# Gathers of two experts' rows moved ahead, and the copy of x to the output in other places, in a fused conditional-linear and mixture-of-experts kernel

## The chip, the core and the metric

The kernel runs on one core of one Trainium2 chip. The metric is the device time of one execution in microseconds (us), and a kernel's time is the median of its runs. Five engines work side by side, each through its own instructions in order: PE (matrix multiply; PEld is its weight load), DVE (elementwise, reductions), ACT (activations, copies), POOL (here mostly indirect DMAs) and SP (here only the issue of DMAs). Each waits for the others by semaphores. DMAs issued by SP, ACT and POOL stand in separate queues and are carried by the same 16 DMA engines. Matrix products are summed in PSUM, everything else lies in SBUF, and inputs, outputs and intermediates in device memory (DRAM).

## The reference, cut to what matters

```python
# x: (4, 1024, 512); per batch row b a category c = itok[b]
xc = einsum('bsd,bdh->bsh', x, W[c]) + b[c]          # conditional linear, (4096, 512)
probs = softmax(xc @ Wr)                             # 8 experts
eidx = argmax(probs); p_tok = probs[eidx]
rank = position of the token among those of its expert   # kept if rank < 512
for e in range(8):                                   # dispatch[e]: up to 512 token numbers
    h  = maximum(xc[dispatch[e]] @ W1[e], 0)         # 512x512 times 512x2048
    ye = (h @ W2[e]) * p_tok                         # 512x2048 times 2048x512
    y[dispatch[e]] += ye
out = x + y
```

All is float32. A token that no expert keeps has `out = x`; a kept token has `out = x + p * ye`.

## The kernel before

**The front (the first 147 us).** The four batch rows are taken in turn. For each, x is loaded in tiles of 512 tokens (`load_x`, L248), turned by PE (`transpose_x`, L268), and multiplied by the category's weight (`load_batch`, L206; `linear`, L473). All products use Strassen's scheme: seven products of half blocks, whose sums and differences DVE forms before and after. The result is written to two DRAM tensors, `xc_dram[0]` and `[1]`, the left and right 256 columns (`done`, L512). Beside it the router picks the expert and the rank of each token; POOL scatters the pairs (probability, token) to `slots` in DRAM, which ACT's queue loads back as `table` (L644), and POOL makes the index tables `src_row` and `dst_row` from it (L651). The loads at the start, all in the order of the program: x tile 0 on ACT's queue (L625), then `wr_sb` (L627) and the zeroing of `slots` (L630) there; on SP's queue the weight of batch row 0 in three pieces (L214), x tile 1, the weight of row 1, x tile 2, the weight of row 2.

**The experts.** Each of the eight experts takes some 95 us. `gather` (L691) brings in rows by indirect DMAs on POOL, in two uses: from pool `xg` (one buffer) the expert's 512 rows of xc, eight DMAs, `rows_of`; from pool `xr` (four buffers) its 512 rows of x itself, four DMAs, `rows`, called the residual here. `fetch(e)` (L711) copies the indices to `at` on DVE and gathers the rows of expert e+1 and the residual of expert e. It is called in `between` (L956) at the second of four groups of hidden columns (g = 1), held behind the latest sum on DVE by `behind`. The rows of expert 0 are gathered at the start of the expert part (L980) and turned on PE (`transpose_rows`, L761). The rows of the later experts are turned without PE: ACT copies them into `strips` (`regroup`, L736, 16 copies), then DVE transposes 32x32 blocks (`turn`, L749) and forms their differences (`sum_xe`, L727).

The first layer (`first_layer`, L781, matmuls L787) makes the hidden values `h` with ReLU on ACT (L807, L814). The second layer (`second_layer`, L840, matmuls L848) makes three big products, k = 1, 6 and 7, into one PSUM bank in turn; the four others are split once more (`inner_product`, L896, matmuls L901). `add` (L828) multiplies a product by the probability and adds it to the residual row (DVE, L833). So product k = 6 cannot write the bank before `add` has read k = 1 out of it, and `add` needs the residual. The last 8 of the 32 matmuls of k = 6 need the last group's sums of `h` (DVE, L163 to L166). The finished rows are scattered to `out` on POOL (L946), and a row buffer of `xr` is free once its scatter has landed.

**The copy of x to the output.** Tokens without an expert need `out = x`, so x is copied to `out` from DRAM to DRAM, 8 MB, before the first scatter. It is in three parts on SP's queue in expert 0, at g = 1, 2 and 3 (L974 to L977), between the loads of the first-layer weights (`load_w1`, L177). `load_w2` (L669) loads an expert's second-layer weight, 4 MB, on the same queue.

**What sets the order.** Inside `tc.manual_schedule` the instructions of PE and SP stand in the order of the program. Those of DVE, ACT and POOL are placed by a scheduler that estimates when each can start; `high_priority` and `issue_after` bend its choice. Each DMA raises one of eight semaphores of its kind, in turn, and a DMA waits until the one before it on its semaphore has landed.

Of the kernel before, what the change touches and what calls it, by code (L numbers as in the profile page):

```python
# [16 lines left out]
P = 128  # L17
# [5 lines left out]
def kernel(  # L23
# [11 lines left out]
    nc = tc.nc  # L35
# [3 lines left out]
    T = B * S  # L39
# [7 lines left out]
    SC = CAP // P  # L47
# [4 lines left out]
    NG = F // (2 * HB * P)  # L52
# [6 lines left out]
    xf = x.rearrange("b s d -> (b s) d")  # L59
    of = out.rearrange("b s d -> (b s) d")  # L60
# [4 lines left out]
    xg = ctx.enter_context(tc.tile_pool(name="xg", bufs=1))  # L65
# [14 lines left out]
    def behind(f, *at):  # L80

        with tc.issue_after(latest[0].ins):
            f(*at)
# [51 lines left out]
    xc_dram = [dram.tile([T, HD], F32, name=f"xc{j}_dram") for j in range(2)]  # L135

    table = const.tile([P, SC, E, ROW], F32, name="table")
    src_row = const.tile([P, NS], I32, name="src_row")
# [53 lines left out]
    with (  # L192
# [55 lines left out]
        def load_x(c, eng=nc.sync):  # L248
            t = xin.tile([P, XT, D], F32, tag="x", name=f"x_{c}")
            n = 1 if c == 0 else XT  # L250
            for j in range(0, XT, n):
                eng.dma_start(
                    out=t[:, j : j + n, :],
                    in_=xf[c * CT + j * P : c * CT + (j + n) * P, :].rearrange(
                        "(j p) d -> p j d", p=P
                    ),
                )
            xrows[c] = t

        def behind_this(f):  # L260
            with tc.issue_after(latest[0].ins):
                latest[0] = f()
# [210 lines left out]
        def linear(b, g, k):  # L473
# [145 lines left out]
            (1, 8): [(load_x, 7)],  # L619
            (1, 12): [(load_w1, 0, 1)],  # L620
            (2, 3): [(load_w1, 0, 2)],
        }

        with tc.manual_schedule(engines={mybir.EngineType.PE, mybir.EngineType.SP}):
# [3 lines left out]
                out=wr_sb[:, :, 0:E], in_=wr.rearrange("(kc p) e -> p kc e", p=P)  # L628
# [16 lines left out]
            out=table.rearrange("p c e r -> p (c e r)"),  # L645
            in_=slots.rearrange("(p s) r -> p (s r)", p=P),
# [13 lines left out]
    xr = ctx.enter_context(tc.tile_pool(name="xr", bufs=SC, reuse_waits="tile"))  # L660
# [6 lines left out]
    rows, residual, xes, hs = {}, {}, {}, {}  # L667
# [23 lines left out]
    def gather(e, pool, sources, into, at):  # L691

        n = D // len(sources)
        if pool is xg:
            into[e, "all"] = pool.tile([P, SC, D], F32, tag="rows", name=f"rows_of_{e}")
        for j, source in enumerate(sources):
            for c in range(SC):
                if pool is xg:
                    into[e * SC + c] = into[e, "all"][:, c, :]
                elif j == 0:  # L700
                    into[e * SC + c] = pool.tile(
                        [P, D], F32, tag="rows", name=f"rows_{e * SC + c}"
                    )
                nc.gpsimd.indirect_dma_start(  # L704
                    out=into[e * SC + c][:, j * n : (j + 1) * n],
                    out_offset=None,
                    in_=source,
                    in_offset=bass.IndirectOffsetOnAxis(ap=at[:, c : c + 1], axis=0),
                )
# [71 lines left out]
    def first_layer(e, g, k):  # L781

        key = (1, e, g)
        ps = bank(ps_p, key, k, [P, HB, HC * P], "h", bufs=2)
        for j in range(HB):
            for kc in range(HK):
                nc.tensor.matmul(  # L787
                    ps[:, j, :],
                    lhsT=w1s[e, g][:, LEFT[k], kc, j * P : (j + 1) * P],
                    rhs=xes[e][:, RIGHT1[k], kc, :],  # L790
                    start=(k in OPENS and j == 0 and kc == 0),
                    stop=(k == LAST[BANK[k]] and j == HB - 1 and kc == HK - 1),
                    skip_group_check=True,
                )
        if e not in hs:
            hs[e] = hp.tile([P, NG, 7, HB, HC * P], F32, tag="h", name=f"h_{e}")
        h = hs[e][:, g, :, :, :]
        if k in (1, 6, 7):
            banks[key, k] = snap.tile(
                [P, HB, HC * P], F32, tag=f"s{k}", bufs=1 + (k == 6), name=f"s{k}_{e}_{g}"  # L800
            )
            snapped[0] = nc.scalar.copy(banks[key, k], ps)  # L802

        def total(into, ps, part):
            with tc.high_priority():
                latest[0] = nc.vector.tensor_tensor(into, ps, part, ALU.add)  # L806
            nc.scalar.activation(into, into, AF.Relu)  # L807

        if k == 2:
            total(h[:, 0, :, :], ps, banks.pop((key, 1)))  # L810
        if k == 7:
            total(h[:, 3, :, :], banks[key, "y"], banks.pop((key, 7)))
        if k == 4:
            nc.scalar.activation(h[:, 1, :, :], ps, AF.Relu)  # L814
        if k == 3:
            total(h[:, 2, :, :], ps, banks.pop((key, 6)))
            sums(nc.vector, *(h[:, i, :, :] for i in range(7)))
# [138 lines left out]
    def between(e, g):  # L956

        if g == 0 and e > 0:
            behind(sum_w1, e, W1G - 2)
        if g > 0:  # L960
            if e > 0 or g > 2:
                first_layer(e, g - 1, 4)
                first_layer(e, g - 1, 3)
            ahead = e * NG + g - 1 + W1G
            if ahead < E * NG:
                load_w1(*divmod(ahead, NG))
            if ahead > W1G and ahead <= E * NG:
                behind(sum_w1, *divmod(ahead - 1, NG))
        part = g - 2 + (e == 0)
        if part in (0, 1):  # L970
            behind(sum_w2, e, part)
        if g == 1:
            behind(fetch, e)
        if e == 0 and g > 0:  # L974

            q = slice((g - 1) * T // (NG - 1) // P * P, g * T // (NG - 1) // P * P)
            nc.sync.dma_start(out=of[q, :], in_=xf[q, :])  # L977

    with tc.manual_schedule(engines={mybir.EngineType.PE, mybir.EngineType.SP}):
        gather(0, xg, xc_dram, rows, src_row)  # L980

        for part, half, then in (
            (0, 0, [(0, 1)]),
            (0, 1, [(1, 1), (0, 5), (1, 5)]),
            (1, 0, [(0, 2)]),
            (1, 1, [(1, 2)]),
        ):
            for c in range(half * HC, (half + 1) * HC):
                transpose_rows(0, c, part)
            for g, k in then:  # L990
                first_layer(0, g, k)

        load_w2(0, xes[0][:, 3, 0, HC * P - 1 :])
        for e in range(E):
            for g in range(NG):
                if e == 0 and g < 2:

                    for k in ((6, 7), (4, 3))[g]:
                        first_layer(e, 0, k)
                        first_layer(e, 1, k)  # L1000
                    between(e, g)
                    continue
                first_layer(e, g, 1)
                first_layer(e, g, 2)
                ahead = range(0 if 0 < e < E - 1 and g == NG - 1 else VB, VB)
                for a in ahead[:1]:
                    regroup(e + 1, a)
                between(e, g)
                for i, k in enumerate((6, 5, 7)):
                    first_layer(e, g, k)  # L1010
                    for a in ahead[i + 1 : i + 2]:
                        regroup(e + 1, a)
            second_layer(e, 1)
            first_layer(e, NG - 1, 4)
            inner_sums(e, 2, sides="right")
            first_layer(e, NG - 1, 3)
            inner_sums(e, 2, sides="left")
            if (e + 1) * NG - 1 + W1G < E * NG:
                load_w1(e + 1, W1G - 1)
            if e == 0:  # L1020

                for a in range(VB):
                    regroup(1, a)

            def small(*turns):
                for k, q in turns:
                    inner_product(e, k, q)

            second_layer(e, 6)
            inner_sums(e, 5)  # L1030
            small(*[(2, q) for q in (1, 5, 2, 6, 3, 7)])
            second_layer(e, 7)
            small((2, 4))
            inner_sums(e, 3)
            inner_sums(e, 4)
            if e + 1 < E:
                turn(e + 1)
            small((5, 5), (5, 2))
            if e + 1 < E:
                sum_xe(e + 1)  # L1040
            small(
                *[(5, 1), (5, 3), (5, 6), (3, 5), (5, 7), (3, 2), (5, 4), (3, 1)],
                *[(4, 5), (4, 1), (3, 6), (4, 2), (4, 6)],
                *[(3, 3), (4, 3), (3, 7), (4, 7), (3, 4), (4, 4)],
            )
            if e + 1 < E:
                load_w2(e + 1)
# [31 lines left out]
```

## Time and profile before

| | us |
|---|---|
| median of 3 runs | 930.53 (929.09 to 930.55) |
| the profiled execution | 935.05 |
| its span, first to last instruction | 933.3 |
| PE busy | 907.0 (97%) |
| DVE busy | 660.2 (71%) |
| ACT busy | 264.1 (28%) |
| POOL busy | 177.6 (19%) |

The profiled execution lies 4.5 us above the median, and 1.75 us of it lie around the span. Times below that name a moment are us from the start of the span. PE is the engine to watch: where it neither multiplies nor waits for its own queue, the kernel stands. The granted clock of PE is listed with the stretches; 1.00 is full speed.

### The profile page before, as it was taken

Reading aid. Unit: us, or ns where it says so; the run is one execution under the profiler, and the core shown is the slowest. Engines: PE = TensorE matmul, PEld = TensorE weight load, DVE = VectorE, ACT = ScalarE, POOL = GpSimd, SP = SyncE. Lnnn points to the kernel's source line nnn. Section 1 sums busy time; section 2 is a strip of 40 time slices with the busy share of each in tenths; the row PEclk is TensorE's granted clock in tenths of the full one; section 3 lists DMA queues with packets and bytes.
Section 4 is the critical chain, followed back from the end, with each engine's and each line's share of the span. In section 5 each row is a group of like instructions: output and inputs, shape, how many; then the busy total and the mean of one; then the engine's idle time right before and its main releaser. Section 6 shows DMA issues by size and latency. Waiting matters only on the chain.

```text
span 933.3 us, 13219 instructions
## 1 busy us (share of the span) xinstructions
PE 907.0 (97%) x5204; PEld 807.8 (87%) x5204; DVE 660.2 (71%) x1226; ACT 264.1 (28%) x506; POOL 177.6 (19%) x173
## 2 busy tenths in 40 slices
PE   9999999986999999999999999999999999999996
PEld 6788787875998899889988998899889988998896
DVE  4656684655946993699469945995599558965893
ACT  3333201315123412351236122602260136013200
POOL 0043343070015001500150015001500150011001
PEclk9999999997999999999999999999999999999999
DMA  9474224991075206520652066205620462135001
GB/s 323 147 232 159 80 92 123 340 376 73 1 241 165 91 1 225 181 91 1 213 187 91 1 201 205 87 5 175 221 71 30 149 227 73 46 120 192 1 1 46
DMA packets 95727, 123.31 MB, mean 132 GB/s; under 512 B 8516, under 2 KB 83268, under 8 KB 95474
## 3 DMA queue, kind: packets, MB, share of 16 engines
q1 hardware_dynamic: 85058, 96.49, 30.9%
q0 software_dynamic: 9216, 24.85, 8.1%
q10 hardware_dynamic: 1392, 1.13, 0.4%
q8 instruction: 41, 0.67, 0.3%
q14 instruction: 20, 0.16, 0.1%
HBM read 105.96 MB, written 25.23 MB: 141 GB/s over the span
## 4 chain that ended last, share of the span: by engine, by line
PE 91%; DVE 3%; DMA 2%; POOL 2%; issue 2%; ACT 1%; POOLq 0%; SPq 0%; DVEq 0%
PE hx L787 22%; PE yx L848 17%; PE yx L901 12%; PE hy L787 11%; PE yy L901 6%; PE xcx_lin L491 6%; PE hz L787 5%; PE yz L901 3%; PE xcy_lin L491 2%; PE xcz_lin L491 1%; POOL rows_of L704 1%; PE ps_xT L276 1%; ACT strips L747 1%; DMA rows<-in_x_dram,at 1%; PE ps_lT L382 1%
## 5 line engine op out<-in xcount | busy, mean ns | idle before, releaser
L787 PE MATMUL hx<-xe,w 128*128 128x256 f32 x1024 | 238.4, 380 | 3.9 <-issue 2.8
L787 PEld LDWEIGHTS hx<-xe,w 128*128 128x128 f32 x1024 | 193.2, 190 | 32.6 <-issue 5.0
L946 POOL DMA_INDIRECT out_dram<-rows,dst_row x32 | 32.0, 999 | 473.5 <-DVE rows L833 421.2
L787 PE MATMUL hy<-xe,w 128*128 128x256 f32 x512 | 120.6, 379 | 0.0
L848 PE MATMUL yx<-w_b,h 128*128 128x256 f32 x512 | 113.1, 379 | 0.0
L802 ACT COPY s<-hx 128x512 f32<-128x512 f32 x96 | 55.7, 580 | 188.5 <-PE hx L787 166.6
L787 PEld LDWEIGHTS hy<-xe,w 128*128 128x128 f32 x512 | 97.3, 190 | 13.2
L848 PEld LDWEIGHTS yx<-w_b,h 128*128 128x128 f32 x512 | 96.7, 190 | 12.8
L806 DVE TENSOR_TENSOR h<-hy,s 128x512 f32<-128x512 f32 x64 | 44.1, 689 | 84.6 <-ACT s L802 38.2
L807 ACT ACTIVATE h<-h 128x512 f32<-128x512 f32 x96 | 60.5, 630 | 114.8 <-DVE h L806 104.3
L704 POOL DMA_INDIRECT rows_of<-xc_dram,at x56 | 63.8, 1140 | 140.7 <-DVE w L164 94.0
L901 PE MATMUL yx<-w_b,h 128*128 128x128 f32 x640 | 84.0, 277 | 0.0
L901 PEld LDWEIGHTS yx<-w_b,h 128*128 128x128 f32 x640 | 79.4, 194 | 1.0
L747 ACT COPY strips<-rows_of 32x512 f32<-32x512 f32 x112 | 69.0, 616 | 16.1 <-DMA rows<-in_x_dram,at 14.7
L848 PE MATMUL yx<-w_t,h 128*128 128x256 f32 x256 | 61.0, 398 | 11.8 <-DVE rows L833 7.1
L848 PEld LDWEIGHTS yx<-w_t,h 128*128 128x128 f32 x256 | 51.2, 201 | 20.1 <-DVE rows L833 7.5
L787 PE MATMUL hz<-xe,w 128*128 128x256 f32 x256 | 60.6, 379 | 0.6 <-DVE xe L769 0.6
L806 DVE TENSOR_TENSOR h<-hz,s 128x512 f32<-128x512 f32 x32 | 22.1, 689 | 54.7 <-PE hz L787 54.7
L787 PEld LDWEIGHTS hz<-xe,w 128*128 128x128 f32 x256 | 48.5, 190 | 7.4 <-DVE xe L769 0.9
L463 POOL DMA_INDIRECT slots<-row,dest x32 | 36.3, 1135 | 95.3 <-DVE dest L459 86.8
L901 PE MATMUL yx<-w_t,h 128*128 128x128 f32 x384 | 51.7, 278 | 0.0
L901 PEld LDWEIGHTS yx<-w_t,h 128*128 128x128 f32 x384 | 46.7, 192 | 0.2
(161 smaller groups left out, 1273.1 us busy)
## 6 DMA issues: line engine op xcount, KB each, us to landing
w<-in_L_ffn_W_dram SPq DMA_DIRECT2D x64, 512.0 KB
w_b<-in_L_ffn_W_dram SPq DMA_DIRECT2D x32, 1024.0 KB
x<-in_x_dram SPq DMA_DIRECT2D x7, 1024.0 KB
xc_dram<-s SPq DMA_DIRECT2D x22, 256.0 KB
out_dram<-in_x_dram SPq DMA_DIRECT2D x2, 2816.0 KB
cw<-in_L_cond_W_dram SPq DMA_DIRECT2D x3, 1024.0 KB
out_dram<-in_x_dram SPq DMA_DIRECT2D x1, 2560.0 KB
xc_dram<-xc SPq DMA_DIRECT2D x8, 256.0 KB
```

Of the source, the lines that this page charges most:

```text
L276: nc.tensor.transpose(ps[:, kc, :], xrows[c][:, j, kc * P : (kc + 1) * P], ident)
L463: nc.gpsimd.indirect_dma_start(out=slots, out_offset=bass.IndirectOffsetOnAxis(ap=dest[:, j : j + 1], axis=0), in_=row[:, j, :], in_offset ...
L491: nc.tensor.matmul(ps[:, j, :], lhsT=left[:, kc, j * P : (j + 1) * P], rhs=right[k][:, kc, :], start=((k in OPENS or (b, k) == (LATE, 3)) ...
L704: nc.gpsimd.indirect_dma_start(out=into[e * SC + c][:, j * n : (j + 1) * n], out_offset=None, in_=source, in_offset=bass.IndirectOffsetOnA ...
L747: nc.scalar.copy(into.rearrange("p k s v -> p s k v"), r[:, :, :, b, :])
L787: nc.tensor.matmul(ps[:, j, :], lhsT=w1s[e, g][:, LEFT[k], kc, j * P : (j + 1) * P], rhs=xes[e][:, RIGHT1[k], kc, :], start=(k in OPENS an ...
L802: snapped[0] = nc.scalar.copy(banks[key, k], ps)
L806: latest[0] = nc.vector.tensor_tensor(into, ps, part, ALU.add)
L807: nc.scalar.activation(into, into, AF.Relu)
L848: nc.tensor.matmul(ps[:, at, :], lhsT=hs[e][:, m // HB, LEFT[k], m % HB, at * P : (at + 1) * P], rhs=w2s[e][RIGHT2[k]][:, m, :], start=(k ...
L901: nc.tensor.matmul(ps, lhsT=left[:, g, :], rhs=right[:, g, :], start=(q in OPENS and g == 0), stop=(q == LAST[BANK[q]] and g == NG - 1), s ...
L946: nc.gpsimd.indirect_dma_start(out=of, out_offset=bass.IndirectOffsetOnAxis(ap=dst_row[:, n : n + 1], axis=0), in_=residual.pop(n), in_off ...
```

## The change

Three things are altered. Expert 0's residual is gathered directly behind the call that gathers its rows, and expert 1's rows behind the first-layer products that follow the turning of expert 0's rows; both read their indices from `src_row`, and `fetch(0)` and its index copy fall away. The copy of x is cut in four parts of 1024 tokens, 2 MB each. The first is written into the plan of the front beside product (2, 5) and issued on ACT's queue. The three others stand on SP's queue after expert 0's first big product and the load of expert 1's third weight block, ahead of `regroup(1)`.

```diff
+        def keep_x(eng, i, n=1):
+
+            q = slice(i * T // 4, (i + n) * T // 4)
+            eng.dma_start(out=of[q, :], in_=xf[q, :])
...
             (2, 3): [(load_w1, 0, 2)],
+            (2, 5): [(keep_x, nc.scalar, 0)],
         }
...
-        if g == 1:
+        if g == 1 and e > 0:
             behind(fetch, e)
-        if e == 0 and g > 0:
-
-            q = slice((g - 1) * T // (NG - 1) // P * P, g * T // (NG - 1) // P * P)
-            nc.sync.dma_start(out=of[q, :], in_=xf[q, :])

     with tc.manual_schedule(engines={mybir.EngineType.PE, mybir.EngineType.SP}):
         gather(0, xg, xc_dram, rows, src_row)
+        gather(0, xr, [xf], residual, src_row)
...
             for g, k in then:
                 first_layer(0, g, k)
+        gather(1, xg, xc_dram, rows, src_row[:, SC : 2 * SC])
...
             if e == 0:
-
+                for i in range(1, 4):
+                    keep_x(nc.sync, i)
                 for a in range(VB):
                     regroup(1, a)
```

## The prediction

> **What bounds the kernel now.** The page gives PE 97% of the span and the chain that ended last 91% PE, so only places where PE stands, or runs slowly, can pay. I went through PE's timeline from the first expert on and compared expert 0 with expert 1, from the first big second-layer product to the next expert's first product. PE's rows (start, duration, count; in brackets the idle time before and what ended it), expert 0:
>
> ```profile
> 195.35 7.07 PE L848 MATMUL yx<-w_b,h 128*128 128x256 f32 x32
> 202.25 1.89 PE L787 MATMUL hx<-xe,w 128*128 128x256 f32 x8
> 203.98 1.89 PE L787 MATMUL hy<-xe,w 128*128 128x256 f32 x8
> 212.94 7.69 PE L848 MATMUL yx<-w_t,h 128*128 128x256 f32 x24 [7.06 <-DVE rows L833]
> 225.32 3.78 PE L848 MATMUL yx<-w_t,h 128*128 128x256 f32 x8 [4.70 <-DVE h L164]
> ...
> 261.94 1.89 PE L787 MATMUL hx<-xe,w 128*128 128x256 f32 x8
> ```
>
> and expert 1, where the same 32 matmuls of k = 6 follow at once:
>
> ```profile
> 307.64 7.07 PE L848 MATMUL yx<-w_b,h 128*128 128x256 f32 x32
> ...
> 318.00 7.07 PE L848 MATMUL yx<-w_t,h 128*128 128x256 f32 x32
> ...
> 356.97 1.89 PE L787 MATMUL hx<-xe,w 128*128 128x256 f32 x8
> ```
>
> Expert 0 takes 66.59 us (261.94 - 195.35), expert 1 49.33: 17.26 us more for the same work. Of these 11.76 are the two idle times (7.06 + 4.70). The rest is a slow clock behind them: the 24 matmuls took 7.69 where 24/32 of 6.91 is 5.18, the 8 took 3.78 for 1.73, and the stretches of 212 to 216 and 224 to 228 us show granted clocks of 0.50 and 0.54.
>
> What is behind the idle times, in the waits from 205 to 226 us (total, times, longest):
>
> ```profile
> ACT strips L747 <- DMA rows<-in_x_dram,at: 14.7, 1, 14.7
> DVE rows L833 <- DMA rows<-in_x_dram,at: 9.2, 2, 8.9
> ...
> DVE xe L754 <- ACT strips L747: 6.9, 1, 6.9
> ```
>
> The first idle time is `add` waiting for expert 0's residual. The second is the 16 `strips` copies, which begin only at 210.87, when the gathers have landed; the transposes on DVE wait for them, and the sums of h stand behind the transposes. The gathers began late (POOL 186.55, held behind DVE's index copy) and then crawled. From 188 to 192 us SP's queue (q1) with its copies of x left POOL's (q0) next to nothing (packets, MB, share of the engines):
>
> ```profile
> q1 hardware_dynamic: 194, 1.82, 109.8%
> q0 software_dynamic: 3, 0.01, 0.7%
> ```
>
> **Step 1, both stalls in expert 0 go.** I read the order of the built program and counted on in the time of before. Residual 0 is issued at about 146 us and expert 1's rows from 160 us on (when PE's last turning of expert 0's rows, at 158.24, frees the one buffer): 8 gathers of about 1.25 (0.95 and 0.30 between) end at 170, some 25 us ahead of their use. `add` then runs at 203, beside PE's two first-layer products (202.25 to 205.71), so k = 6 starts at 205.71 and wants its last 8 matmuls' sums at 205.71 + 5.18 = 210.89. On ACT `strips` starts behind the snapshot ending at 196.19: 3 copies (0.626 each, as 8.14 for 13), a ReLU 0.63, 12 copies 7.51, a ReLU 0.60, one copy 0.61: 207.4. From the last strip to the end of the DVE sum that PE needs (L164) took 225.27 - 222.16 = 3.11 before, so 210.6. That is 0.3 inside. What is late next is thus ACT's strips, with almost no margin; I charge 0.2. Gain **17.26 - 0.2 = 17.1**, and at worst 12 if strips or transposes come 3 to 5 us late and PE's clock drops once more.
>
> **Step 2, the front pays for the first copy.** The plan has it beside product (2, 5), but ACT's order is the scheduler's, and the built program has it in fourth place on ACT: behind the zeroing of `slots` (issued at 3.38) and ahead of ACT's table load (3.76). So it is issued at about 3.8 us. There the DMA engines are full (busy of PE, PEld, DVE, ACT, POOL, then clock, DMA share, GB/s):
>
> ```profile
> 6.00:8.00 2.00, 1.64 (x13) 1.09 (x11) 0.00 (x0) 1.65 (x4) 0.00 (x0) 1.00 0.98 307
> 8.00:10.00 2.00, 1.78 (x8) 1.58 (x9) 0.69 (x1) 0.49 (x2) 0.00 (x0) 1.00 0.99 342
> ...
> 26.00:28.00 2.00, 2.00 (x17) 1.16 (x18) 0.69 (x1) 0.89 (x2) 0.00 (x0) 1.00 1.05 408
> ```
>
> 2.1 MB at the 380 to 410 GB/s of 12 to 28 us is 5.1 to 5.5 us. Its 32 rows of 64 KB are larger pieces than the 44 KB that left q0 0.7%, so I let it hold the engines alone for 5.2 us, from about 7 (ACT's queue still has small packets at 6 to 8), and shift every load on SP's queue by that. The first 256 KB of weights, for which PE waits at 8.22, is just in. The third piece of weights, for which DVE waited 0.91 us until 10.12, comes at 15.3; four DVE operations of 0.61 behind it let PE's third product start at 17.8 in place of 13.53. x tile 1 was first used at 16.38, was in by 15.8 at the latest (SP's next load on its semaphore was issued then), and comes by 21.0 against 16.38 + 4.3 = 20.7. PE is nearly gapless from there to 147 us, so the delay stays: **+4.4**. If the loads keep their share it is 0, and all of 5.2 plus a slow clock is 8.6 at most (rival B).
> x tile 2's load also waits for the copy, which holds the place before it on its semaphore: issued near 14 instead of 9.98 and first used at 31.74, it has room. ACT's own issue (0.66 to 4.70 for the copies before) holds its first copy of `xT` (6.09) 0 to 4 us; PE loses that once, ahead of the weights it waits for anyway.
>
> **Step 3, POOL's new order.** The residual gathers stand between the two halves of expert 0's rows. They wait for the front's last matmul (146.3, its operands lie where the buffers are) and take 4 x 1.25, so the second half, which began at 150.11, starts at 151.35 or, with 1 MB more in the air, 152.5. It was used at 155.18 with no wait. A landing of 2.7 us (last write of `xc_dram` issued by 147.4, seen by POOL at 150.11) gives 155.3 for the second gather that this needs: **+0.6**, 0 to 2.5.
> Then POOL has expert 2's rows ahead of expert 0's scatter, and expert 1's residual behind it. From expert 1's start they came at 17.7 and 28.6 us; now 17.7, scatter 28.6, residual from 33.7 on, landed near 42. Its first `add` is at 52.6 (314.7 - 262.1): hidden by 10 us.
>
> **Step 4, what moves under cover.** The three copies are issued at about 207, take 6.3 MB / 380 GB/s = 17 us while DMA is idle (216 to 260 us: 0 to 4 GB/s), and are done 20 us before `load_w2(1)`. Expert 1's rows (1 MB) now share 160 to 175 us with `load_w2(0)`: about 3 us later, at 178, where DVE first uses it at 178.11, and then w1 of group 3 at 180.5 against its use at 183.25. The index copy (0.16) goes. Cost nothing, at worst 1.
>
> **Sum.** -17.3 + 0.2 + 4.4 + 0.6 = -12.1. The profiled execution becomes 935.05 - 12.1 = 922.9. It stood 4.5 above the median; with the same distance the median is 930.53 - 12.1 = **918.4**.
>
> **A rule weighed.** By the row above a queue beside large copies keeps 0.7%, and the sum goes by it. The Trainium skill, DMA: Bandwidth & Descriptors, section Queues, rings and completion order, has each DMA engine take turns between queues and drain some 9 to 17 descriptors at a turn. An estimate by that page: a turn of 1 KB pieces carries up to 17 KB against 64, so the loads keep a fifth, the weights come 4.2 late in place of 5.2, and the sum would be -13.1.
>
> **Rivals.**
> A: the front's copy costs little (0 to 2), because the loads keep their share or the copy truly runs later. For it: DMA moves 0 GB/s at 38 to 42 us, and the plan names row 2. Against: the built order. Sum -15.7, so 914.8.
> B: the front's stall also slows PE's clock. PE would stand from 10.0 to about 13.8. A 4.70 us idle time was followed by a half clock, and 3.78 and 1.91 for 1.73 and 0.89 is about 3.4 us lost in all. Sum -8.7, so 921.8. The Trainium skill, TensorE: Matmul & The Clock Gate, section HAM oscillation, puts the limit of a harmless gap at about 3.4 us; no row here shows a gap between 1 and 4.7 behind the start.
> C: a stall is left in expert 0, since margins of 0.3 are as thin as I can count. Step 1 at 12: sum -7, so 923.5.
> D, slower: the first copy creeps. x tile 2 waits for it, and SP's queue stands behind that load. A landing after 26 us makes it late (1 MB at 400 GB/s and 2.7 to land are 5.3, and it is needed at 31.74). This delay takes the place of step 2's, so the kernel is slower than before from a landing at 26.4 + 17.1 - 0.6 = 43 us, which is 55 GB/s. At 40 GB/s it lands near 57, 31 late: -17.1 + 0.6 + 31 = +14.5, 945. Against: while the copies of before ran, DMA moved 290 GB/s or more (184 to 208 us).
>
> **Chances.** Forecast (916 to 920.5) 0.53, A 0.18, B 0.15, C 0.10, D 0.04. With D, the outer third of A and the outer half of C left out, 8 in 10 lie in 913.8 to 924.0. A measurement tells about 0.2% (1.9 us) from no change; faster by more 0.94, within 0.02 (the worst of B and C together), slower 0.04 (D).
>
> **What would show it.** Step 1: no idle time of PE between 205 and 226 us (shifted by the front) and 49.3 to 49.8 us from k = 1 to expert 1. Step 2: a big DMA on ACT's queue within the first 5 us, PE waiting for `cw` and x tile 1 between 10 and 21, and the first product of the expert part about 4.4 later than 147.73. Step 3: residual gathers between the halves, and PE waiting up to 2.5 us at the second half's transposes; no wait for the residual in expert 1. It is wrong if ACT's queue issues the copy near 100 us, or if PE waits anywhere new after 262.

## The result and the profile after

The changed kernel takes **922.53 us** (median of 4 runs, 921.73 to 923.01) against 930.54 for the kernel before on the same chip: ratio 0.9915, 95% interval [0.9898, 0.9932]. That is 8.0 us faster where 12.1 were forecast. The profiled execution took 921.73, its span 920.0.

PE's rows from k = 1 of expert 0 to the first product of expert 1, in the changed kernel (start, duration, count; in brackets the idle time before and what ended it; L854 was L848, L907 was L901):

```profile
201.17 7.07 PE L854 MATMUL yx<-w_b,h 128*128 128x256 f32 x32
...
209.80 1.89 PE L793 MATMUL hy<-xe,w 128*128 128x256 f32 x8
211.53 7.07 PE L854 MATMUL yx<-w_t,h 128*128 128x256 f32 x32
...
236.06 1.16 PE L907 MATMUL yx<-w_t,h 128*128 128x128 f32 x8 [0.34 <-DVE p L88]
...
251.39 0.81 PE L793 MATMUL hx<-xe,w 128*128 128x256 f32 x3
```

Product k = 6 (211.53) follows the first-layer products at once, as 32 matmuls in one row: both idle times of before (7.06 and 4.70) are gone. From k = 1 to expert 1 it is 251.39 - 201.17 = 50.22 where it was 66.59. The waits of the same stretch (211 to 232 us; total, times, longest) name no gather any more; of the strips chain 0.8 is left, on DVE:

```profile
ACT p L936 <- PE yx L907: 7.2, 2, 5.7
DVE xe L760 <- ACT strips L753: 0.8, 1, 0.8
...
```

The front has become longer. PE's rows there:

```profile
9.90 0.38 PE L335 MATMUL ps_wT<-ident,cw 128*128 128x128 f32 x2
14.20 0.87 PE L335 MATMUL ps_wT<-ident,cw 128*128 128x128 f32 x6 [3.92 <-DMA cw<-in_L_cond_W_dram]
14.91 3.04 PE L496 MATMUL xcz_lin<-cw,xT 128*128 128x256 f32 x8
17.75 1.61 PE L335 MATMUL ps_wT<-ident,cw 128*128 128x128 f32 x8
19.19 1.89 PE L496 MATMUL xcx_lin<-wd,xs 128*128 128x256 f32 x8
```

PE stands 3.92 us for the second piece of the weights, and then eight matmuls take 3.04 where the same eight in the third product take 1.89: a slow clock. The third product starts at 19.19 where it was 13.53, and the first expert product at 153.39 where it was 147.73: 5.66 later, all of it lost by 19.19. The DMA queues say why, in 8 to 10 us and then in 10 to 12 us (packets, MB, share of the engines; q10 is ACT's, with the copy of x, q1 is SP's, with the weights):

```profile
q10 hardware_dynamic: 30, 1.05, 123.6%
q1 hardware_dynamic: 159, 0.16, 22.8%
```

```profile
q10 hardware_dynamic: 16, 1.05, 123.2%
q1 hardware_dynamic: 16, 0.02, 2.3%
```

The stretches (busy of PE, PEld, DVE, ACT, POOL, then clock, DMA share, GB/s) show PE idle and then at half clock:

```profile
10.00:12.00 2.00, 0.28 (x3) 0.05 (x1) 0.00 (x0) 0.00 (x0) 0.00 (x0) 1.00 1.26 532
...
16.00:18.00 2.00, 2.00 (x7) 1.48 (x6) 2.00 (x4) 0.00 (x0) 0.00 (x0) 0.50 0.42 103
```

DVE stands for the third piece. Four of its operations behind that piece, `wd`, `xs`, `wd` and `s`, come before the third product, the first and the last of them here:

```profile
16.00 0.69 DVE L306 TENSOR_TENSOR wd<-cw 128x512 f32<-128x512 f32 x1 [6.98 <-DMA cw<-in_L_cond_W_dram]
...
17.81 0.69 DVE L510 TENSOR_TENSOR s<-xcx_lin,cb 128x512 f32<-128x512 f32 x1
```

Last, expert 1 has two idle times that before did not have, 0.17 at 295.76 and this one:

```profile
291.90 1.97 PE L793 MATMUL hx<-xe,w 128*128 128x256 f32 x8 [0.63 <-DVE w L164]
```

**The theory put to the test**: the change is three things. Expert 1's rows ahead of time are the gain; the first copy of x in the front costs a wait and a slow clock behind it; and something in expert 1 costs 1.3. The rivals: that the copies in expert 0, not the late gathers, were what made before stall, and that before's extra time lay elsewhere.

### The profile page after: what moved, and what is told of

It is laid out like the page before. It is cut to its first block, busy times and chain, and to the rows that moved or that the text cites. A ratio compares the mean times of both kernels' runs of the same rounds, so it can differ in the third digit from the quotient of the medians.

```text
span 920.0 us, 13223 instructions
## 1 busy us (share of the span) xinstructions
PE 902.8 (98%) x5204; PEld 805.5 (88%) x5204; DVE 660.5 (72%) x1225; ACT 264.8 (29%) x506; POOL 173.2 (19%) x173
## 4 chain that ended last, share of the span: by engine, by line
PE 89%; DVE 6%; ACT 1%; DMA 1%; issue 1%; POOL 0%; POOLq 0%; SPq 0%; ACTq 0%; DVEq 0%
PE hx L793 23%; PE yx L854 14%; PE hy L793 11%; PE yx L907 11%; PE xcx_lin L496 6%; PE hz L793 6%; PE yy L907 5%; PE yz L907 3%; PE xcy_lin L496 2%; PE xcz_lin L496 2%; PE ps_xT L281 1%; DMA cw<-in_L_cond_W_dram 1%; ACT strips L753 1%; PE ps_wT L335 1%; PE ps_lT L387 1%
## 5 line engine op out<-in xcount | busy, mean ns | idle before, releaser
L854 PE MATMUL yx<-w_b,h 128*128 128x256 f32 x512 | 113.1, 379 | 0.0
L854 PEld LDWEIGHTS yx<-w_b,h 128*128 128x128 f32 x512 | 96.7, 190 | 12.8
L710 POOL DMA_INDIRECT rows_of<-xc_dram,at x48 | 50.2, 1046 | 185.8 <-DVE w L164 173.0
L907 PE MATMUL yx<-w_b,h 128*128 128x128 f32 x640 | 83.2, 275 | 0.0
L907 PEld LDWEIGHTS yx<-w_b,h 128*128 128x128 f32 x640 | 78.5, 192 | 0.8
L854 PE MATMUL yx<-w_t,h 128*128 128x256 f32 x256 | 56.6, 379 | 0.0
L854 PEld LDWEIGHTS yx<-w_t,h 128*128 128x128 f32 x256 | 48.6, 190 | 6.6
L907 PE MATMUL yx<-w_t,h 128*128 128x128 f32 x384 | 51.9, 278 | 0.5 <-DVE p L88 0.3
L907 PEld LDWEIGHTS yx<-w_t,h 128*128 128x128 f32 x384 | 46.6, 192 | 1.3 <-DVE p L88 0.8
```

The costliest lines, as they stand in the source:

```text
L710: nc.gpsimd.indirect_dma_start(out=into[e * SC + c][:, j * n : (j + 1) * n], out_offset=None, in_=source, in_offset=bass.IndirectOffsetOnA ...
L854: nc.tensor.matmul(ps[:, at, :], lhsT=hs[e][:, m // HB, LEFT[k], m % HB, at * P : (at + 1) * P], rhs=w2s[e][RIGHT2[k]][:, m, :], start=(k ...
L907: nc.tensor.matmul(ps, lhsT=left[:, g, :], rhs=right[:, g, :], start=(q in OPENS and g == 0), stop=(q == LAST[BANK[q]] and g == NG - 1), s ...
```

## The experiments

Three stretches of each profiled execution carry most of what follows: the start of the first expert product; from k = 1 of expert 0 to expert 1 (the block); and from the start of expert 1 to the first-layer product behind its k = 1.

| kernel | median us | first expert product | block | in expert 1 |
|---|---|---|---|---|
| before, first profile | 930.54 | 147.73 | 66.59 | 52.61 |
| before, again (b_again) | 930.38, one run | 147.88 | 66.08 | 51.80 |
| the change | 922.53 | 153.39 | 50.22 | 53.11 |
| e1_copy_row3 | 917.82 | 149.53 | 50.25 | 53.11 |
| e2_gathers_only | 914.45 | 147.27 | 50.23 | 51.80 |
| e3_copies_only | 933.59 | 147.49 | 70.26 | 53.12 |
| e4_copies_late | 915.72 | 147.39 | 50.24 | 53.10 |
| e5_front_small_pieces | 923.73 | 154.35 | 50.24 | 53.11 |
| e6_residual_ahead | 931.81 | 147.32 | 67.32 | 51.80 |
| e7_rows_ahead | 914.23 | 146.89 | 50.23 | 51.80 |
| e8_copies_next_expert | 925.37 | 147.52 | 61.25 | 51.81 |
| e9_front_half | 917.86 | 149.54 | 50.23 | 53.10 |

The kernel before, timed beside them, moved from call to call between 929.81 and 931.11, so changed kernels are compared by their own times and these stretches.

### b_again: the kernel before, unchanged

> The kernel before, unchanged, profiled a second time. Question: the profiled executions moved by 13.3 us of span (933.3 to 920.0), the medians by 8.0 (930.54 to 922.53). Theory S (the stalls vary): the two waits in expert 0 depend on when gathers land beside the copies and on where the clock's windows fall, so this execution has a shorter block from the first big second-layer product to expert 1 than 66.59 us (61 to 65), and a span near 928.5. Theory T (elsewhere): the block is again 66 to 67 us and the five small PE gaps of 0.5 to 0.6 us in the later experts, which the changed kernel did not show, come and go instead.

930.38, and the block is 66.08 again, with 8.21 and 3.55 us of idle time in the places where the first profile had 7.06 and 4.70. What came and went is small: the first profile had five idle times of PE of 0.52 to 0.58 in experts 1 to 6, with nothing named behind them but "issue", some 0.8 us each (expert 1's stretch was 52.61, now 51.80). Five times 0.8, and the 0.5 of the block, is about the 4.5 us by which that execution lay above the median. So it was right to forecast the median by a difference and not from that execution; that the profile of the change would stand as far above its own median was not (it lies 0.8 below). What makes these idle times come and go stays open.

### e2_gathers_only: gathers ahead, copies of x where they were

```
# against the changed kernel
-            (2, 5): [(keep_x, nc.scalar, 0)],
+        if e == 0 and g > 0:
+            q = slice((g - 1) * T // (NG - 1) // P * P, g * T // (NG - 1) // P * P)
+            nc.sync.dma_start(out=of[q, :], in_=xf[q, :])
-                for i in range(1, 4):
-                    keep_x(nc.sync, i)
```

> Only the gathers are moved ahead; the copy of x stays in its three parts at g = 1, 2 and 3 of expert 0 on SP's queue as before. Theory (gathers issued at 146 to 174 us are out of the copies' way, and the front has no copy): no PE idle time in expert 0, block 50.2, front as before, so 922.5 - 5.7 = 916.8. Rival (the copies hold up something else, such as expert 1's first weights or POOL's order): 920 to 930.

**914.45**, ratio 0.9821 [0.9808, 0.9835], 16.5 under the 930.99 of before on the same chip. The block is 50.23 with the copies in their old places, so early gathers need nothing moved out of their way, and this half of the change is better than the whole of it by 8.1 us.

### e3_copies_only: the copies behind k = 1, gathers as before

```
# against the changed kernel
-            (2, 5): [(keep_x, nc.scalar, 0)],
-        gather(0, xr, [xf], residual, src_row)
-        gather(1, xg, xc_dram, rows, src_row[:, SC : 2 * SC])
-        if g == 1 and e > 0:
+        if g == 1:
             behind(fetch, e)
-                for i in range(1, 4):
+                for i in range(4):
                     keep_x(nc.sync, i)
```

> Only the copy is moved: all four parts of 2 MB on SP's queue behind expert 0's first big product, none in the front; the gathers stay in fetch(0), held until 186 us. Theory (the copies' large pieces, not the late issue, made the gathers crawl): POOL's gathers take 1.25 each, expert 1's rows land near 199, the residual near 204, strips end near 209.5 in place of 222.2, PE idles 1 to 2 us in expert 0, median 917 to 919. Rival (the late issue alone makes the stall): the two idle times stay near 7 and 5 us, median 928 to 930.5.

**933.59**, ratio 1.0027 [1.0017, 1.0037]: a little slower than before, and above what either theory of the pair expected. The residual now meets the copies in full. PE's row and its longest wait, then the queues in 212 to 216 us (q0 is POOL's with the residual):

```profile
224.75 8.81 PE L853 MATMUL yx<-w_t,h 128*128 128x256 f32 x32 [19.13 <-DVE rows L838]
```

```profile
q1 hardware_dynamic: 16, 1.05, 68.2%
q0 software_dynamic: 17, 0.07, 4.3%
```

The residual's last gather is issued at 208.99, the copies from 206.62 on, and k = 6 starts only at 224.75. So moving the copies by themselves does not help: issued while the late gathers are under way, they starve the last of them. The counts show how. In 216 to 220 and 220 to 224 us they are 48 and 47, then 32 and 32 packets (2.10 and 0.19 MB, then 1.05 and 0.07): the engines took one packet of each queue in turn, and one of the copies' is 64 KB where one of the residual's is 2 to 4 KB.

### e8_copies_next_expert: gathers as before, no copy near them

```
# against the kernel before
-        if e == 0 and g > 0:
+        if e == 1 and g > 0:
             q = slice((g - 1) * T // (NG - 1) // P * P, g * T // (NG - 1) // P * P)
```

> The kernel before with its copies of x moved one expert on, to the same places in expert 1; all gathers as late as before. Theory L (the late issue is the main cause, the copies add to it): POOL begins at 186.5 again and the first gathers again take 1.8 to 5.6 us, since they did so without any copy near them when all copies came after k = 1; expert 1's rows land at 207 at the latest, the residual issued at about 205 to 210 lands by 212, PE waits 5 to 7 us ahead of k = 6 and 2 to 4 behind it, block 60 to 64, time 924 to 928. Rival (the copies are the cause): with a free DMA the gathers are in by 203, block 50 to 52, time 914.5 to 916.5.

(Its copies run after expert 0's scatters and overwrite some of what those wrote; only its time is read here.) **925.37**, ratio 0.9936 [0.9921, 0.9952], block 61.25: as the theory had it (60 to 64, 924 to 928). Of the 15.9 us by which before's block (66.08) exceeds 50.23, late issue alone makes 61.25 - 50.23 = 11.0 and the copies of x add 4.8. The rival of this pair, that the copies are the cause, falls; so does half of the prediction's picture of gathers that "crawled" behind the copies. POOL took as long, and longer, with no copy there (the third gather 5.57, in before 3.17). What the copies do is in the transfers: q0 moved 48 packets in 188 to 192 us, where it had 3 in before. POOL's rows (the idle time before in brackets), with one from the early gathers of e2_gathers_only to compare:

```profile
186.34 1.81 POOL L704 DMA_INDIRECT rows_of<-xc_dram,at  x1 [31.62 <-DVE w L163]
...
191.99 5.57 POOL L704 DMA_INDIRECT rows_of<-xc_dram,at  x1 [0.30 <-issue]
```

```profile
162.75 0.94 POOL L709 DMA_INDIRECT rows_of<-xc_dram,src_row  x1 [0.30 <-issue]
```

### e6_residual_ahead and e7_rows_ahead: which gather it is

```
# both against e2_gathers_only; e6:
-        gather(1, xg, xc_dram, rows, src_row[:, SC : 2 * SC])
# e7:
-        gather(0, xr, [xf], residual, src_row)
# in both, the gather taken out is back in fetch(0), as before
```

> The kernel before with only expert 0's residual gathered ahead; expert 1's rows and the copies of x stay where they were. Theory (the two idle times of expert 0 are two chains, and the one through strips sets the end): the wait of `add` (7.06 in before) goes, but the strips still begin at 207 to 210.9 when expert 1's rows have landed, so PE only stands later, for the sums of the last 8 products: one idle time of 10 to 14 us ahead of them, expert 0 from k = 1 to expert 1 in 62 to 66 us in place of 66.1 to 66.6, time 926 to 930. Rival (each idle time is worth its own length): block 58 to 59, time 922 to 923.

> The kernel before with only expert 1's rows gathered ahead; expert 0's residual stays behind the late copy of indices, and the copies of x stay. Theory: the strips chain is free, and the residual, now first in POOL's order, is issued from 186.5 to about 197 (1.81, 3.23, 3.17, 1.02 and the steps between, as the first four gathers of before) and lands at 200 to 210 beside the copies, while `add` wants it at 203: an idle time of 0 to 5 us ahead of k = 6 and none behind it, block 50.2 to 57, time 914.5 to 921. Rival (copies starve it whatever its place): the 7 to 8 us stay, block 59 to 61, time 923.5 to 925.5.

With the residual alone ahead: **931.81**, ratio 1.0004 [0.9995, 1.0014]; with expert 1's rows alone: **914.23**, ratio 0.9818 [0.9803, 0.9833]. PE's rows at k = 6, first e6_residual_ahead, then e7_rows_ahead:

```profile
206.01 5.34 PE L854 MATMUL yx<-w_t,h 128*128 128x256 f32 x24
226.81 3.78 PE L854 MATMUL yx<-w_t,h 128*128 128x256 f32 x8 [15.46 <-DVE h L164]
```

```profile
204.87 7.07 PE L853 MATMUL yx<-w_t,h 128*128 128x256 f32 x32
```

The first idle time of before was in the shadow of the second. Take away the wait for the residual, and PE waits 15.46 in one place in place of 7.06 + 4.70 in two, for the sums of h that stand behind the transposes of expert 1's rows; the block even grew (67.32, and the time with it, a little past the 62 to 66 and the 926 to 930 expected). Take away the wait for those rows, and the whole 16 us go: the residual, now first in POOL's order (185.24 to 195.86), is there when `add` wants it, with the copies still beside it.

### e4_copies_late, e1_copy_row3, e9_front_half, e5_front_small_pieces: the front

```
# each against the changed kernel, cut; e4:
-            (2, 5): [(keep_x, nc.scalar, 0)],
-                for i in range(1, 4):
+                for i in range(4):
# e1:
+            (2, 5): [(keep_x, nc.sync, 0)],
# e9:
+            (2, 5): [(keep_x, nc.scalar, 0, 0.5)],
+                keep_x(nc.sync, 0.5, 0.5)
# e5, where of_x and to are the slices of xf and of, for the copy in the front alone:
+                to, of_x = (t.rearrange("(a p) d -> p a d", p=P) for t in (to, of_x))
```

> The changed kernel with no copy in the front: all four copies on SP's queue behind k = 1 of expert 0, gathers ahead as in the change. Theory: against the kernel with the gathers alone (914.45) it differs only in expert 1, where the scheduler put DVE's weight sums in another order (PE gaps of 0.63 and 0.17, expert 1 in 53.1 in place of 51.8): first expert product at 147.0 to 147.5, k = 1 to expert 1 50.2, time 915.3 to 916.3; so the front copy's whole price is 922.5 - 915.8 = 6.7 us, 5.7 of it by the third product. Rival (four copies issued at one place cost something of their own, as 6.3 MB against 8.4 MB): any new idle time of PE between 202 and 245, time above 917.5.

**915.72** (915.46 to 915.94), ratio 0.9847 [0.9833, 0.986]: inside the 915.3 to 916.3. The front copy's price is thus 922.53 - 915.72 = **6.8**, and four copies behind k = 1 make no new wait in expert 0. Against e2_gathers_only it is 1.3 slower, and so are the stretches in expert 1 (53.10 and 51.80). In the table every kernel with copies behind k = 1 has 53.10 to 53.12 there, and every one without them 51.80 or 51.81, but for the first profile of before with its idle time behind "issue". DVE's order differs between the two: with the copies behind k = 1 the scheduler puts the sums of the second-layer weight (L170 to L173, four of 1.22 us) ahead of four sums of `w` that PE wants first; in e2_gathers_only those are done before three of the four. DVE's rows in e4_copies_late, and PE's that waits for the second:

```profile
283.25 1.22 DVE L173 TENSOR_TENSOR w_t<-w_b,w_t 128x1024 f32<-128x1024 f32 x1
...
285.10 0.69 DVE L164 TENSOR_TENSOR w<-w 128x512 f32<-128x512 f32 x1
```

```profile
285.94 1.97 PE L792 MATMUL hx<-xe,w 128*128 128x256 f32 x8 [0.63 <-DVE w L164]
```

> The changed kernel with one word altered: the first copy is issued by SP in place of ACT, so that it really stands beside product (2, 5), near 100 us. Theory (the copy at 4 us starves the first loads and costs 5.7 us of PE): the first product of the expert part is back at 147.7 (153.4 in the changed kernel), no half clock in the front, expert 0's block stays at 50.2, and the median is 922.5 - 5.7 = 916.8. Rival (the front is late for another reason, such as the altered order on DVE): 922.5. Rival (the copy costs as much near 100 us, where DMA is loaded by 80 to 123 GB/s): 918 to 922.

With the first copy truly at (2, 5), on SP's queue at 103.00: **917.82**, ratio 0.9854 [0.9839, 0.9869], 4.7 better than the change where 5.7 were expected. Most of the missing part is again an order and not the transfer: PE has one new idle time, late in the front,

```profile
132.20 1.99 PE L496 MATMUL xcx_lin<-wd,xs 128*128 128x256 f32 x8 [1.54 <-DVE s L510]
```

and on DVE six sums of `w` (from 127.86 us on) stand ahead of the `s` that PE wants there; in e2_gathers_only such an `s` follows after two (128.68). That is 1.54 of the 2.1 by which its first expert product is later than in e4_copies_late; the other 0.6 is not explained.

> The changed kernel with half of the first copy (1 MB, 16 pieces of 64 KB) in its place in the front and the other half with the copies behind k = 1. DVE's order is that of the changed kernel. Theory (the front pays by bytes, and a gap of PE near 4 us costs a half clock on top): the third piece of weights comes 2.6 us late in place of 5.7, PE's gap ahead of the first weight transposes is 1 to 2 us, its clock stays whole, the third product starts at 16 to 16.5 in place of 19.2, the first expert product at 149.8 to 150.5, time 918.7 to 920. Rival (what counts is that a large piece stands at the head of each engine's queue, however many follow): third product at 18 or later, time above 921.

**917.86**, ratio 0.9869 [0.9854, 0.9884], a little under the 918.7 to 920 expected. DVE's row for the third piece of weights, then PE's rows:

```profile
12.69 0.69 DVE L306 TENSOR_TENSOR wd<-cw 128x512 f32<-128x512 f32 x1 [3.15 <-DMA cw<-in_L_cond_W_dram]
```

```profile
12.80 1.06 PE L335 MATMUL ps_wT<-ident,cw 128*128 128x128 f32 x8 [0.27 <-DMA cw<-in_L_cond_W_dram]
15.24 1.99 PE L496 MATMUL xcx_lin<-wd,xs 128*128 128x256 f32 x8 [1.38 <-DVE s L510]
```

The third product is 2.06 later than in e4_copies_late (13.18), the clock stays at 1.00, and the price is 917.86 - 915.72 = 2.1. The price is less than the delay of the weights: with no copy in the front DVE begins on the third piece at 10.19, and its four operations end at 12.75, 0.43 before PE comes to the third product. Half a copy delays the piece by 12.69 - 10.19 = 2.50, and 2.50 - 0.43 is the 2.06. The whole copy delays it by 16.00 - 10.19 = 5.81; by the same count the third product would start at 18.55, right behind the `s` that ends at 18.50. It starts at 19.19, since PE is still busy with the slow rows before it (3.04 for 1.89 and 1.61 for 1.04). These rows lose 1.7, but 1.1 of it is time in which PE would have waited for DVE. So of the change's 19.19 - 13.18 = 6.0 the late weights are 5.4, and the slow clock is 0.6.

> The changed kernel with one alteration: the first copy of x, still on ACT's queue at the start, goes in pieces of 2 KB (one row each) in place of 64 KB (32 rows). Same bytes, same place, same instruction count. Theory P (the size of the piece decides what the loads on SP's queue keep beside it, as 22.8 % and 2.3 % of the engines in 8 to 12 us in the changed kernel): with pieces as small as the loads' own, the loads keep about half, the third piece of weights comes 2 to 3 us late in place of 5.7, PE's gap stays under 3 us and its clock does not drop, so the first expert product is at 149.5 to 151 in place of 153.4 and the time is 918.5 to 920.5. Rival Q (bytes ahead in the engines decide, whatever the piece): third product at about 19.2 again, first expert product 153.4, time 922.5.

**923.73**, ratio 0.9915 [0.99, 0.9929]: no better than the change. The loads did keep more (q1 in 10 to 12 us, beside the copy in 2 KB pieces, where the change had 2.3%; again the two queues have about as many packets):

```profile
q10 hardware_dynamic: 251, 0.51, 67.3%
q1 hardware_dynamic: 250, 0.26, 36.9%
```

but the copy then stayed about twice as long (8 to 15.5 us, where the change has all of it in 8 to 12), since it moved 0.5 MB in 2 us where 64 KB pieces moved 1.05. The third piece of weights is 4.19 late in place of 5.81, and PE's rows show two shorter waits and a longer half clock:

```profile
14.38 0.69 DVE L309 TENSOR_TENSOR wd<-cw 128x512 f32<-128x512 f32 x1 [5.15 <-DMA cw<-in_L_cond_W_dram]
```

```profile
14.49 1.06 PE L338 MATMUL ps_wT<-ident,cw 128*128 128x128 f32 x8 [1.83 <-DMA cw<-in_L_cond_W_dram]
17.42 3.78 PE L499 MATMUL xcx_lin<-wd,xs 128*128 128x256 f32 x8 [1.86 <-DVE s L513]
21.13 1.90 PE L351 MATMUL ps_wr<-wT,wr_sb 128*32 128x512 f32 x8
```

Theory P was right on the shares and on earlier weights, and wrong on the clock: the third product starts at 17.42, 1.8 before that of the change, but now the half clock falls behind the last wait, where DVE's waits hide none of it, and the rows it slows (3.78 for 1.89 and 1.90 for 1.06) lose 2.7. The rival, that bytes decide whatever the piece, has the time but not the cause: it expected the third product at 19.2.

## Why the prediction was right, and where not

The sign held, and so did the range of 8 in 10 (913.8 to 924.0), but not the band of the forecast (916 to 920.5). The time came out 4.1 above the forecast. That it lies near rival B's 921.8 is luck: B's slow clock is 0.6 of these 4.1 where B had 3.4; the weights came later than charged, and DVE's order in expert 1 cost 1.3. By steps, each with the runs that isolate it:

| step | predicted | measured | by |
|---|---|---|---|
| 1 and 3, gathers ahead | -17.1 + 0.6 = -16.5 | -16.5 | e2_gathers_only |
| 4, copies behind k = 1 | 0, at worst 1 | +1.3 | e4 against e2 |
| 2, first copy in the front | +4.4 | +6.8 | the change against e4 |
| sum | -12.1 | -8.4 (-8.0 direct) | |

(The first row is against 930.99, the kernel before beside that run; the direct one against 930.54. Such differences between calls are all that parts the two sums.)

**Step 1** held in its mechanism and, with some luck, in its size: by the profiles of b_again and e2 the block gives 66.08 - 50.23 = 15.85, step 3 takes back 0.25 (first expert product to k = 1, 47.61 and 47.86), and another 0.6 is a front that ended earlier in e2's (147.88 and 147.27), which no step claims. The strips were forecast to end at 207.4, which with the later start of the change (201.17 - 195.35 = 5.82) is 213.2; they end at 213.20. No idle time is left between k = 1 and k = 6. The block is 50.22 where 49.33 + 0.2 was forecast. The 0.7 more in the block is not late strips at k = 6, as the step had it, but DVE further on: it works without a break from 226 us, and PE waits for it in the small products (the row at 236.06). Within the step one reading was wrong without harm to the sum: the two idle times were taken as a sum of two, while e6 shows that the first is worth nothing by itself; and of the late arrival, 4.8 us are the copies and 11.0 the late and slow issue.

**Step 2** is the step that failed in size. The place was right (fourth on ACT's queue, issued at 3.94), and so was the mechanism: the weights came late, PE and DVE waited for them, and x tile 1 then came without a wait at 22.05. Two terms were too small. The step let the copy hold the engines for 5.2 us, and so had the third piece of weights at 15.3 and the third product at 17.8; the piece came at 16.00, which alone would put the product at 18.55. And the sum had nothing for the slow clock, which stood only in rival B; it moved the product on to 19.19, 0.6 and not B's 3.4: the slow rows lose 1.7, and 1.1 of that falls where PE would have waited for DVE. e9, with waits of 0.27 and 1.38, shows the front without a slow clock. (The profiles give 6.0 for the front against e4, the medians 6.8; the change's profiled execution lies 0.8 below its median, and where the others lost that is not known.) On the rule weighed there: the Trainium skill, DMA: Bandwidth & Descriptors, section Queues, rings and completion order, has the engines take turns between queues. The trace agrees with the turns, but by its counts a turn is one packet: 16 beside 16 in the change, 251 beside 250 in e5, 48 beside 47 in e3, and not the 9 to 17 of the estimate. So in 10 to 12 us the loads moved 0.02 MB beside the copy's 1.05, not a fifth, and the third piece of weights came 5.9 late and not 4.2.

**Step 3**: 47.78 from the first expert product to k = 1 against 47.62 before, 0.2 where 0.6 was charged (the residual gathers were issued at 152.22 to 155.96, and the second half was in time). No wait for the residual appears in expert 1.

**Step 4** counted the transfers, which are free as forecast, and not the scheduler. DVE's instructions were neither added nor taken away in expert 1, but their order there is computed from estimated times, and moving DMAs on SP's queue changed it: 1.3 us. The step had no term for DVE's order.

**What would be better**: the gathers alone, or expert 1's rows alone (914.45 and 914.23), beat both kernels.

## What to carry to other kernels

When two waits follow one another, ask which of the two chains ends last: removing the earlier one can be worth nothing, as the residual was here, and removing the later one everything. A transfer put ahead of the first loads delays them, here by 2.5 us for 1 MB and 5.8 for 2 MB, and 4.2 for 2 MB in small pieces, which did not pay since PE's clock then dropped at a worse place. What a slow clock costs is not the sum of its slow rows: take off what PE would have waited anyway. The transfers put where the DMA engines stood idle cost nothing by themselves. With a scheduler in between, every move of a DMA is also a move of instructions on engines that the diff does not touch: compare the built order of each of them.

## What the runs showed of the hardware

- Two queues with work waiting were served one packet for one (16 and 16 in 10 to 12 us of the change, 251 and 250 there in e5, 48 and 47 in 216 to 220 of e3), so what each got went by the size of its pieces. Pieces of 64 KB took the engines almost alone: 1.05 MB in 2 us with 2.3 to 22.8% left for the queue beside them. Pieces of 2 KB moved 0.47 to 0.51 MB in 2 us and left 34.8 to 40.2%.
- One idle time of 3.92 us brought a half clock; the drop came when PE was already at work again (1.00 from 10 to 14 us, 0.87 from 14 to 16, 0.50 from 16 to 18). So did two of 1.83 and 1.86 with 1.06 us of matmuls between (granted clock 0.50 from 18 to 22 us in e5_front_small_pieces); 0.27 and 1.38 did not. The Trainium skill, TensorE: Matmul & The Clock Gate, section HAM oscillation, warns of single gaps over some 3.4 us; by these rows shorter ones close together do it too.
- A gather's issue on POOL took 0.94 at 162.75 in e2_gathers_only and 1.81 to 5.57 at 186 to 198 in e8 and e3, which had no copies there. DVE was busy 4.00 of 4 us from 192 to 196 in e8, mostly with sums whose two operands lie in SBUF, and 2.22 of 4 us at 160 to 164 in e2_gathers_only. The Trainium skill, SBUF — State Buffer, section Who interferes with whom, has such sums contend with POOL instructions that read SBUF. These rows agree, but in e2_gathers_only an issue at 277.33 took 0.95 with such sums running on DVE throughout, so they are not enough by themselves. No run here took DVE's sums away: the cause is not shown.
